# Edge attention on a graph: four batches to a period, Q and E by edge, and one tie of the gathers to TensorE per period

## The chip, the cores and the metric

The kernel runs on one core of one Trainium2 chip. The time is device microseconds of one execution. Engine names are those of the profile: PE is TensorE's matmuls and PEld its weight loads, DVE is VectorE, ACT is ScalarE, POOL is GpSimd, and SP is SyncE, which here only issues DMAs. POOL issues the gathers, each an indirect DMA that fetches one row for each of 128 partitions.

## The reference

A graph has 6250 nodes with 128 features and 206250 edges, sorted by their destination `dst`. Every edge has 128 features of its own. With 8 heads of 16 features:

```python
Qh = (h @ WQ).reshape(N, H, D)
Kh = (h @ WK).reshape(N, H, D)
Vh = (h @ WV).reshape(N, H, D)
Eh = (edge_attr @ WE).reshape(-1, H, D)
score = jnp.einsum('ehd,ehd,ehd->eh', Kh[src], Qh[dst], Eh) * inv_sqrt_d
score = jnp.exp(jnp.clip(score, -5.0, 5.0))
msg = Vh[src] * score[:, :, None]
wV = jax.ops.segment_sum(msg, dst, num_segments=N)
Z = jax.ops.segment_sum(score, dst, num_segments=N)
h_out = wV / (Z[:, :, None] + 1e-06)
```

The output is `layernorm(x + h_out)` over the features. So for every edge, the row of K and V of its source is needed, the row of Q of its destination, and E of the edge. All data are float32.

## The kernel before

**Tiles.** The edges are cut into 1612 tiles of 128 edges, and these into 406 batches: 401 of four tiles, then five smaller ones. A batch `b` goes through stages, and each turn of the main loop (lines 464 to 516) works on several batches at different stages.

**Head.** `table` (lines 226 to 245) computes K and V of all nodes in 49 blocks of 128: one matmul into PSUM each (`kvacc`), a copy by ACT or DVE into `kvst`, and stores into the table `kv` in HBM. `q_rows` computes Q, split into three bfloat16 parts that add up to the float32 value, and stores it in `qs`. While the table is not there yet, the first 12 batches (`XB`) gather rows of `x` (512 bytes) instead of rows of `kv` (1 KB), and `project` computes their K and V on the spot.

**Stages of a batch.**
- `gather` (line 307): POOL issues four indirect DMAs into a tile `kvrows`; there are 17 such tiles (`GB`).
- `stage_0`: DVE compares each edge's destination with a row of numbers. `onehot` has the edges on the partitions, `onehotT` has the Q rows of a window of 42 nodes (times three parts) on them, in bfloat16.
- `stage_a`: PE multiplies the window's Q rows with `onehotT` (`qps`, line 354), one product of 512 columns, whose result has the features on the partitions and the edges along the row. ACT copies it to SBUF (`qT`, line 356). PE multiplies the edge features with WE in the same layout (`eps`, line 358).
- `pairs`: DVE multiplies `qT` with `eps` (`eq`, line 365). `turn`: PE transposes the four tiles of `eq` to have the edges on the partitions (`pps`, line 373).
- `stage_b`: DVE multiplies the gathered K rows with `pps` (`kq`, line 379), sums over each head (line 382) and clips (line 385). `weigh`: ACT takes the exponential twice, once into PSUM (`bank`) for the messages and once into the last eight columns of `msg`.
- `messages`: DVE multiplies the gathered V rows with the weights (`msg`, line 413). `stage_c`: PE multiplies `onehot` with `msg` and adds this up in PSUM over a group of 11 tiles (`agg`, line 431). After a group ACT copies the sum out (`sum`, line 441).
- When the groups that touch 128 nodes are there, `finish` adds them by PE with shifted identity matrices (`finps`, line 401), and `layernorm` makes some 17 small DVE operations, of which `fill()` issues one at a time between the others.

**What sets the order.** From batch 12 on, every engine keeps to the order of the program (`manual_schedule`). A float32 product is two instructions on PE. The gathers are tied to PE: the first of the four of batch `b`, from batch 16 on, waits for the `qps` product of batch `b - lag(b)`, where `lag` falls from 12 to 1 within the first 60 batches:

```python
if i == 0 and b >= LOCK:
    tc.add_manual_dep(ins.ins, expanded[b - lag(b)].ins.name, ...
```

SP's queue holds the loads of edge features (`ea`, 512 KB for 8 tiles), of the Q windows (`qw`), of `relb` (the destinations for `onehotT`), and the stores of the table, of Q and of the output.

Of the kernel before, what the change touches and what calls it, by code (L numbers as in the profile page):

```python
# [8 lines left out]
F32 = mybir.dt.float32  # L9
# [18 lines left out]
GB = 17  # L28
XB = 12
LOCK = XB + 4  # L30
STEP = 1
# [3 lines left out]
AHEAD = 2  # L35
EB = 6
SLAG = 2
# [6 lines left out]
QLOOK = 3  # L44
# [30 lines left out]
def q_built(j):  # L75

    return min(NB, (j * N // NJ + 3 * P - 1) // P)


@with_exitstack  # L80
def edge_attention(ctx: ExitStack, tc: tile.TileContext, x, xT, srcT, dstT, dstB, dst0, bnd, lo, eaT,
# [30 lines left out]
    with ExitStack() as fast:  # L112
# [78 lines left out]
        def count_inside():  # L191
# [9 lines left out]
            nc.vector.tensor_copy(cnt_i, pc)  # L201
# [5 lines left out]
        psE = fast.enter_context(tc.tile_pool(name="psE", bufs=1, space=bass.MemoryType.PSUM))  # L207
        psQ = fast.enter_context(tc.tile_pool(name="psQ", bufs=1, space=bass.MemoryType.PSUM))
        psP = fast.enter_context(tc.tile_pool(name="psP", bufs=2, space=bass.MemoryType.PSUM))
# [4 lines left out]
        bank = psX.tile([P, P + B * H], F32, name="bank")  # L214
        iota_p, exp_p = bank[:, :P], bank[:, P:].rearrange("p (b h) -> p b h", h=H)
        nc.vector.tensor_copy(iota_p, iota_f)

        def pair_bank(i, name, shape):

            pool, tag = ((psE, "eps"), (psP, "pps"), (psQ, "qps"), (psP, "pps"))[i % 4]  # L220
            return pool.tile(shape, F32, name=name, tag=tag)
# [4 lines left out]
        def table(b0):  # L226
            st = wp.tile([P, KB, 2 * D], F32, name="kvst", bufs=2)
            blocks = range(b0, min(NB, b0 + KB))
            for b in blocks:
                n = min(P, N - b * P)  # L230
                ps = pair_bank(b, "kvacc", [P, 2 * D])
                nc.tensor.matmul(ps[:n], xT_sb[:, LEFT + b * P:LEFT + b * P + n], wkv_sb,
                                 start=True, stop=True)
                if b % 2:
                    nc.vector.tensor_copy(st[:n, b - b0, :], ps[:n])
                else:
                    nc.scalar.copy(st[:n, b - b0, :], ps[:n])
# [5 lines left out]
            if len(full) < len(blocks):  # L243
                b = blocks[-1]
                nc.sync.dma_start(kv[b * P:N], st[:N - b * P, b - b0, :])

        batches = cut_batches()
        nbat = len(batches)
        manual = []
        xbs, stores, norms, pending, ready = {}, [], [], [], []  # L250
# [4 lines left out]
        def q_rows(q):  # L255
            n = min(P, N - q * P)
            ps = psT.tile([P, D], F32, name="qrows", tag="oT")
            nc.tensor.matmul(ps[:n], xT_sb[:, LEFT + q * P:LEFT + q * P + n], wq_sb, start=True, stop=True)
            st = wp.tile([P, QP, D], BF16, name="qst", bufs=1)
            r1 = wp.tile([P, D], F32, name="qr1", bufs=1)  # L260
            nc.scalar.copy(st[:n, 0, :], ps[:n])  # L261
            nc.vector.tensor_tensor(r1[:n], ps[:n], st[:n, 0, :], op=ALU.subtract)  # L262
            nc.scalar.copy(st[:n, 1, :], r1[:n])
            nc.vector.tensor_tensor(st[:n, 2, :], r1[:n], st[:n, 1, :], op=ALU.subtract)
            nc.sync.dma_start(qs[q * P * QP:(q * P + n) * QP].rearrange("(p s) f -> p s f", s=QP), st[:n])
            built.append(q)

        def load_q(j):
            if j >= NJ or j in loaded:
                return  # L270
            if j % QREG == 0:
# [4 lines left out]
            loaded[j] = wp.tile([QROWS, D], BF16, name="qw", bufs=QLOOK + 2)  # L276
            nc.sync.dma_start(loaded[j], qs[ds(regs[j % QREG], QROWS), :])

        def load_rel(c):
# [3 lines left out]
            rels[c] = wp.tile([QROWS, RC * P], BF16, name="relb", bufs=2)  # L283
# [3 lines left out]
        chunks, aggs, sums, st8, expanded = {}, {}, {}, {}, {}  # L287
# [9 lines left out]
        def ea_tiles(t, n):  # L297

            load_chunk(t // CH)
            j = t % CH * P  # L300
            return chunks[t // CH][:, j:j + n * P]

        def lag(b):

            return max(STEP, 12 - (b - LOCK) // 4)

        def gather(b):
            rows, f = (x, D) if b < XB else (kv, 2 * D)
            g = gp.tile([P, B, 2 * D], F32, name="kvrows")
            for i, t in enumerate(batches[b]):  # L310
# [6 lines left out]
                if i == 0 and b >= LOCK:  # L317
                    tc.add_manual_dep(ins.ins, expanded[b - lag(b)].ins.name,
# [4 lines left out]
        def project(g, n):  # L323
# [4 lines left out]
            xgT = wp.tile([P, B, P], F32, name="xgT", tag="kq", bufs=2)  # L328
            nc.scalar.copy(xgT[:, :n], pt[:, :n])
            for i in range(0, n, 2):  # L330
                k = min(2, n - i)
                pk = pair_bank(i // 2, "kvps", [P, 2, 2 * D])
# [4 lines left out]
        def stage_0(b):  # L337
            t0, n = batches[b][0], len(batches[b])
            oh = wp.tile([P, B, P], F32, name="onehot", bufs=AHEAD + 5)
# [328 lines left out]
```

## Time and profile before

Three executions took 2434.01, 2427.33 and 2426.94 us; the median is 2427.33 us.

| what | value |
|---|---|
| profiled execution | 2430.0 us, of which the profile's span is 2428.1 us |
| PE busy | 1539.8 us, 63% |
| DVE busy | 1577.4 us, 65% |
| POOL busy | 1534.0 us, 63% |
| ACT busy | 458.9 us, 19% |
| granted TensorE clock, mean | 0.811 |
| moved by DMA | 398.16 MB, mean 164 GB/s |

A line of the groups names the source line, the engine, the operation, its output and inputs with their shapes, and how often it ran; then the busy time in us, the mean of one in ns, and the engine's idle time just before these instructions with what ended most of it. "issue" is time in which an engine waited for nothing that the profile shows, and "remote" is a wait whose releaser it can't name. A line of the waits has, after the engine, the line and what ended the wait: us in total, times, and the longest in us.

### The profile page before, as it was taken

To read this page: it belongs to the slowest core of one execution; us is meant where nothing else is said; L and a number is where in the kernel's file an instruction comes from. 1 tells how busy PE (TensorE), PEld (TensorE's weight loads), DVE (VectorE), ACT (ScalarE), POOL (GpSimd) and SP (SyncE) were. 2 spreads that over 40 slices of the span, in tenths; PEclk is the share of its full clock that TensorE was granted. 3 is DMA by queue.
4 is the path that set the end of the run, shared out by engine and by line. 5 is a ranking of instruction groups with operands and counts; after the bars stand their busy time and mean duration, and the time that the engine had idled before them with its cause. 6 is when DMAs were issued, how large, how long until landed. Compare 5 with 4: busy or idle time off the path is not lost.

```text
span 2428.1 us, 24930 instructions
## 1 busy us (share of the span) xinstructions
PE 1539.8 (63%) x6880; PEld 1086.0 (45%) x6880; DVE 1577.4 (65%) x3779; ACT 458.9 (19%) x1572; POOL 1534.0 (63%) x1619
## 2 busy tenths in 40 slices
PE   3587666666665666657666666666666656656665
PEld 2365444444444444444444444444444444444444
DVE  1368778666766666667667666666666667666766
ACT  0232122111111111111111111111111111111111
POOL 7346565666666666666666666666666666666664
PEclk6898898887878888778877878788778788887887
DMA  5645555556554555556456554655555556554642
GB/s 176 201 144 174 179 156 178 165 150 185 170 166 148 168 177 156 164 152 196 147 157 196 160 156 149 184 168 151 169 162 178 147 155 196 157 156 146 197 150 71
DMA packets 178482, 398.16 MB, mean 164 GB/s; under 512 B 61756, under 2 KB 87526, under 8 KB 178336
## 3 DMA queue, kind: packets, MB, share of 16 engines
q0 software_dynamic: 76592, 208.18, 29.4%
q1 hardware_dynamic: 100604, 187.38, 25.2%
q8 instruction: 57, 0.93, 0.2%
q10 hardware_dynamic: 1140, 0.93, 0.1%
q14 instruction: 89, 0.73, 0.1%
HBM read 381.54 MB, written 14.81 MB: 163 GB/s over the span
## 4 chain that ended last, share of the span: by engine, by line
PE 34%; another core or an unknown queue 23%; DVE 19%; issue 16%; ACT 4%; DMA 2%; POOL 1%; DVEq 1%; SPq 0%; ACTq 0%; POOLq 0%
PE agg L431 10%; PE eps L358 10%; PE pps L373 7%; DVE sc L382 4%; DVE kq L379 4%; DVE eq L365 3%; PE qps L354 3%; ACT qT L356 2%; DVE msg L413 2%; PE finps L401 2%; POOL kvrows L314 1%; DVE onehot L340 1%; DVE onehotT L344 1%; DMA kvrows<-kv,src 1%
## 5 line engine op out<-in xcount | busy, mean ns | idle before, releaser
L314 POOL DMA_INDIRECT kvrows<-kv,src x1564 | 1487.1, 951 | 862.3 <-issue 385.6
L431 PEld LDWEIGHTS agg<-msg,onehot 128*128 128x128 f32 x3224 | 516.7, 230 | 664.3 <-issue 520.9
L431 PE MATMUL agg<-msg,onehot 128*128 128x136 f32 x3224 | 560.5, 326 | 352.8 <-DVE msg L413 137.2
L373 PE MATMUL pps<-shift,eq 128*128 128x128 f32 x1612 | 320.5, 332 | 419.6 <-DVE eq L365 238.5
L365 DVE TENSOR_TENSOR eq<-qT,eps 128x512 f32<-128x512 f32 x406 | 276.4, 681 | 476.2 <-ACT qT L356 210.9
L358 PE MATMUL eps<-ea,we_sb 128*128 128x512 f32 (+1 forms) x812 | 528.2, 738 | 16.8 <-issue 13.4
L373 PEld LDWEIGHTS pps<-shift,eq 128*128 128x128 f32 x1612 | 221.4, 168 | 477.4 <-DVE eq L365 282.4
L356 ACT COPY qT<-qps 128x512 f32<-128x512 f32 x406 | 236.8, 583 | 1048.5 <-remote 428.8
L379 DVE TENSOR_TENSOR kq<-kvrows,pps 128x512 f32<-128x512 f32 x406 | 274.8, 677 | 12.1 <-remote 3.5
L413 DVE TENSOR_TENSOR msg<-kvrows,bank 128x512 f32<-128x512 f32 x406 | 274.6, 676 | 9.8 <-ACT bank L391 4.3
L382 DVE TENSOR_REDUCE sc<-kq 128x32 f32<-128x512 f32 x406 | 276.0, 680 | 7.3
L340 DVE TENSOR_TENSOR onehot<-bank,dst_sb 128x512 f32<-128x512 f32 x406 | 275.8, 680 | 0.0
L358 PEld LDWEIGHTS eps<-ea,we_sb 128*128 128x128 f32 x812 | 192.1, 238 | 50.0 <-issue 14.6
L354 PE MATMUL qps<-onehotT,qw 126*128 126x512 bf16 x406 | 187.3, 461 | 0.9 <-ACT qT L356 0.9
L344 DVE TENSOR_SCALAR onehotT<-relb,node 126x512 bf16<-126x512 bf16 x406 | 147.0, 363 | 16.7 <-remote 11.2
L391 ACT ACTIVATE bank<-sc 128x32 f32<-128x32 f32 x406 | 83.0, 204 | 257.2 <-DVE onehot L340 139.8
L401 PEld LDWEIGHTS finps<-sum,shift 128*128 128x128 f32 x478 | 73.1, 215 | 62.4 <-issue 33.9
L401 PE MATMUL finps<-sum,shift 128*128 128x136 f32 x478 | 75.8, 307 | 30.9 <-ACT sum L441 26.2
L262 DVE TENSOR_TENSOR qr<-qrows,qst 128x128 f32<-128x128 f32 (+1 forms) x49 | 14.2, 289 | 116.8 <-ACT qst L261 104.4
L393 ACT ACTIVATE msg<-sc 128x32 f32<-128x32 f32 x406 | 88.0, 217 | 0.0
L385 DVE TENSOR_SCALAR sc<-sc 128x32 f32<-128x32 f32 x406 | 79.2, 195 | 7.3
L441 ACT COPY sum<-agg 128x136 f32<-128x136 f32 x146 | 39.3, 269 | 236.2 <-remote 100.7
(66 smaller groups left out, 525.9 us busy)
## 6 DMA issues: line engine op xcount, KB each, us to landing
ea<-eaT SPq DMA_DIRECT2D x201, 512.0 KB
relb<-relD SPq DMA_DIRECT2D x100, 504.0 KB
kvrows<-kv,src POOLq DMA_INDIRECT x1564
qw<-qs SPq DMA_DIRECT2D x202, 31.5 KB
kv<-kvst SPq DMA_DIRECT2D x12, 512.0 KB
qs<-qst SPq DMA_DIRECT2D x48, 96.0 KB
xb<-x SPq DMA_DIRECT2D x48, 64.0 KB
out<-h SPq DMA_DIRECT2D x48, 64.0 KB
```

Of the source, the lines that this page charges most:

```text
L314: ins = nc.gpsimd.indirect_dma_start(out=g[:k, i, :f], out_offset=None, in_=rows, in_offset=bass.IndirectOffsetOnAxis(ap=src_col(t)[:k], a ...
L340: nc.vector.tensor_tensor(oh[:, :n], iota_p[:, None, :].to_broadcast([P, n, P]), rel[:, t0:t0 + n, None].to_broadcast([P, n, P]), op=ALU.i ...
L354: expanded[b] = nc.tensor.matmul(pq[:, :n * P], loaded[t0 // WT], ohT[:, :n * P], start=True, stop=True)
L356: nc.scalar.copy(qT[:, :n * P], pq[:, :n * P])
L358: nc.tensor.matmul(pe[:, :n * P], we_sb, ea_tiles(t0, n), start=True, stop=True)
L365: nc.vector.tensor_tensor(eq[:, :n * P], qT[:, :n * P], pe[:, :n * P], op=ALU.mult)
L373: nc.tensor.transpose(pp[:, i, :], eq[:, i * P:i * P + P], ident)
L379: nc.vector.tensor_tensor(t1[:, :n], g[:, :n, :D], pp[:, :n], op=ALU.mult)
L382: nc.vector.tensor_reduce(sc[:, :n], t1[:, :n].rearrange("p b (h d) -> p b h d", h=H), axis=AX.X, op=ALU.add)
L401: nc.tensor.matmul(ps, shift[:, P - s:2 * P - s], sums[k], start=i == 0, stop=stop and i == len(parts) - 1)
L413: nc.vector.tensor_tensor(m[:, :n, :D].rearrange("p b (h d) -> p b h d", h=H), g[:, :n, D:].rearrange("p b (h d) -> p b h d", h=H), exp_p[ ...
L431: nc.tensor.matmul(aggs[k], oh[:, i, :], m[:, i, :], start=first and not final, stop=last)
```

## The change

The main loop takes **periods** of four batches (100 of them, for batches 0 to 399), then periods of one batch for the last six. Within a period:

1. `multiply` for each of the four batches: DVE multiplies the gathered K rows with the Q product and then the result with the E product, both read from PSUM. After each, `expand(b + 2)` orders PE's products for the batch two further on.
2. `weigh`, `messages` and `aggregate` for the four batches, one step apart.
3. `one_hot` for the four batches of the next period, and `one_hot_rows` for four batches.

Q and E are computed **by edge**: in `expand`, `onehotT` and the edge features are the stationary operands, tile by tile, and the results have the edges on the partitions. The copy `qT`, the multiply `eq` with it, and the transposes `pps` are gone. PSUM has two buffers each for `qps` and `eps`.

The gathers have **one tie a period**: the first of its 16 waits for the last `agg` product of the period `p - lag(p)`; from period 4 on, with lag 4 at first and 2 from period 12 on. There are 14 gather tiles in place of 17. The **x gathers**, 48 in number, are tied to `table`'s products from the third batch on. Three groups of sums share a PSUM bank and are copied out at once. The Q rows and the sums of 128 nodes are jobs: their PE products are ordered after the multiplies of a period, and the copies behind them in the next one. Stores are issued a period later; `ea` has 5 buffers in place of 6, `relb` 3 in place of 2.

```diff
-GB = 17
+GB = 14
 XB = 12
-LOCK = XB + 4
-STEP = 1
+PER = 4
+LOCK = XB // PER + 1
+STEP = 2
...
+        def lag(p):
+            return max(STEP, 4 - (p - LOCK) // 4)
+        def gather(b, p=0, made=None):
...
-                if i == 0 and b >= LOCK:
-                    tc.add_manual_dep(ins.ins, expanded[b - lag(b)].ins.name,
+                if i == 0 and p >= LOCK and b == periods[p][0]:
+                    made = added[p - lag(p)]
+                if i == 0 and made is not None:
+                    tc.add_manual_dep(ins.ins, made.ins.name,
...
+        def expand(b):
             t0, n = batches[b][0], len(batches[b])
             if b < XB:
-                project(g, n)
-            oh, ohT = st8.pop(b)
-            pq = psQ.tile([P, B * P], F32, name="qps")
-            expanded[b] = nc.tensor.matmul(pq[:, :n * P], loaded[t0 // WT], ohT[:, :n * P], start=True, stop=True)
-            qT = wp.tile([P, B * P], F32, name="qT", bufs=2)
-            nc.scalar.copy(qT[:, :n * P], pq[:, :n * P])
-            pe = psE.tile([P, B * P], F32, name="eps")
-            nc.tensor.matmul(pe[:, :n * P], we_sb, ea_tiles(t0, n), start=True, stop=True)
+                project(gathered[b], n)
+            ohT = hotT.pop(b)
+            pq = psQ.tile([P, B, D], F32, name="qps")
+            for i in range(n):
+                nc.tensor.matmul(pq[:, i, :], ohT[:, i * P:i * P + P], loaded[t0 // WT], start=True, stop=True)
+            pe = psE.tile([P, B, D], F32, name="eps")
+            for i in range(n):
+                nc.tensor.matmul(pe[:, i, :], ea_tile(t0 + i), we_sb, start=True, stop=True)
+            pairs[b] = pe, pq
...
+            nc.vector.tensor_tensor(t1[:, :n], g[:, :n, :D], pq[:, :n], op=ALU.mult)
+            fill()
+            nc.vector.tensor_tensor(t1[:, :n], t1[:, :n], pe[:, :n], op=ALU.mult)
...
-        gathered = {b: gather(b) for b in range(min(XB, len(batches)))}
+        gathered = {b: gather(b) for b in range(2)}
         for b0 in range(0, NB, KB):
-            table(b0)
+            made = table(b0)
...
+            for b in range(len(gathered), min(XB, nbat)):
+                if (b - 2 if b < 5 else b) * KB > b0:
+                    break
+                gathered[b] = gather(b, made=made)
...
+            for b in c:
+                multiply(b)
+                step()
+                if b + EA < nbat:
+                    expand(b + EA)
+            while job:
+                step()
+            if p == 15:
+                pc = count_inside()
+            else:
+                new_job(c)
+            for i in range(len(c) + 1):
+                if i < len(c):
+                    weigh(c[i], i)
+                    fill()
+                if i:
+                    messages(c[i - 1], i - 1)
+                    aggregate(c[i - 1], p)
+                    fill()
...
+            for b in periods[p + 1] if p + 1 < len(periods) else ():
+                one_hot(b)
+                fill()
+            while next_row[0] < min(nbat, c[-1] + 1 + EA + (len(periods[p + 1]) if p + 1 < len(periods) else 0)):
+                one_hot_rows(next_row[0])
+                next_row[0] += 1
+                fill()
```

## The prediction

> **What bounds the kernel now.** I read the busy line first, then the chain, the costliest groups, all waits by engine, and last the timelines of POOL, ACT and PE side by side.
>
> ```profile
> PE 1539.8 (63%) x6880; PEld 1086.0 (45%) x6880; DVE 1577.4 (65%) x3779; ACT 458.9 (19%) x1572; POOL 1534.0 (63%) x1619
> ...
> PE 34%; another core or an unknown queue 23%; DVE 19%; issue 16%; ACT 4%; DMA 2%; POOL 1%; DVEq 1%; SPq 0%; ACTq 0%; POOLq 0%
> ...
> L314 POOL DMA_INDIRECT kvrows<-kv,src x1564 | 1487.1, 951 | 862.3 <-issue 385.6
> L431 PE MATMUL agg<-msg,onehot 128*128 128x136 f32 x3224 | 560.5, 326 | 352.8 <-DVE msg L413 137.2
> L373 PE MATMUL pps<-shift,eq 128*128 128x128 f32 x1612 | 320.5, 332 | 419.6 <-DVE eq L365 238.5
> L358 PE MATMUL eps<-ea,we_sb 128*128 128x512 f32 (+1 forms) x812 | 528.2, 738 | 16.8 <-issue 13.4
> L356 ACT COPY qT<-qps 128x512 f32<-128x512 f32 x406 | 236.8, 583 | 1048.5 <-remote 428.8
> L379 DVE TENSOR_TENSOR kq<-kvrows,pps 128x512 f32<-128x512 f32 x406 | 274.8, 677 | 12.1 <-remote 3.5
> ```
>
> No engine is full by its busy share, and 23% of the chain has no releaser that the profile knows. The gathers decide. Each of the 1564 from the kv table takes 0.951 us, and the next one starts 0.306 us after it even when nothing is late:
>
> ```profile
> POOL kvrows L314 <- issue: 399.9, 1306, 1.0
> ...
> POOL kvrows L314 <- DMA relb<-relD: 32.5, 1, 32.5
> ```
>
> 399.9 / 1306 = 0.306, so a gather costs 1.257 us. Busy 1487.1, plus 1564 x 0.306 = 479, plus 351 of longer pauses is 2317 us, and the POOL timeline shows just that stretch: from 96.2 (after the 32.5 us wait for the table) to 2412.2. The 351 us are what can be won there. The POOL timeline has 171 such pauses (gaps above 0.6 us): 351 / 171 = 2.05 us each beyond the usual gap, after runs of mostly 12, 8 or 4 gathers. Why POOL pauses is seen in three timelines of one stretch (start, us, engine, instruction, idle before):
>
> ```profile
> 1193.44 0.38 PE L354 MATMUL qps<-onehotT,qw 126*128 126x512 bf16 x1
> ...
> 1200.54 0.63 PE L354 MATMUL qps<-onehotT,qw 126*128 126x512 bf16 x1
> ```
> ```profile
> 1197.41 0.59 ACT L356 COPY qT<-qps 128x512 f32<-128x512 f32 x1 [4.93 <-remote]
> ...
> 1204.54 0.59 ACT L356 COPY qT<-qps 128x512 f32<-128x512 f32 x1 [6.30 <-PE agg L431]
> ```
> ```profile
> 1201.40 0.95 POOL L314 DMA_INDIRECT kvrows<-kv,src  x1 [0.31 <-issue]
> 1204.77 0.94 POOL L314 DMA_INDIRECT kvrows<-kv,src  x1 [2.43 <-PE agg L431]
> ```
>
> The product of 1193.44 has ended at 1193.82, but ACT's copy starts 3.6 us later; that of 1200.54 is picked up at 1204.54, 2.3 us after POOL went still, and POOL itself, tied to that product, goes on at the same moment. So TensorE's results are learned of late by the others while gathers are issued back to back, and all at once some 2.3 us after the gathers stop. By the same comparison 198 of the 406 qps copies start over 1 us after their product. No such lateness is seen between DVE and ACT. The cause I can't read from the trace; the regularity I use.
>
> **The change, part by part.** (1) *One tie per 16 gathers instead of one per 4.* A period is 16 x 1.257 = 20.1 us of gathers. If each tie ends a run, it costs 2.1 us (row above): 22.2 us a period, where four batches now take 2317 / 391 x 4 = 23.7. From below, a tie already met costs nothing (20.1). From above, DVE decides (rival C). I take the pause: the nearest rows are the runs of 12, which nearly all end in one. 97 periods carry kv rows: 97 x 20.1 = 1951, 97 x 2.1 = 204.
>
> (2) *Is the work of a period hidden under its gathers?* DVE is busy 1577.4 / 406 x 4 = 15.5 us per four batches. The edit keeps its count: eq (681 ns, qT from SBUF) becomes a second multiply (g x Q, then x E: nearest row 677), reduce, clip, messages, one-hots and layernorm steps are the same. What is new is where it stands. TensorE's Q and E of a period's batches 0 and 1 are ordered in the period before; those of 2 and 3 only behind the multiplies of 0 and 1. After 16 gathers, DVE finishes multiplies 2 and 3 (2 x 1.36 us), then does weights, messages and one-hots of the period (some 10 us), then multiplies 0 and 1 of the next: about 15.5 us into the next run. Batches 2 and 3 then need TensorE results that, late as now, come 2.3 us after the run ends. DVE stands from 15.5 to 22.2 and goes on: its loop closes in the same 22.2 us. The last sum (added) of that period lies about 11 us into a run; the tie with lag 2 asks for it at the end of that run, so nothing waits longer. Queued behind the waiting multiply on DVE is the whole weigh stage, and behind it ACT's Exp and PE's sums; all fit in. Cost: nothing, hidden by 20.1 us of gathers; without that cover it is rival C.
>
> (3) *TensorE.* Gone: 1612 transposes, 320.5 us. The E product becomes 3224 half-instructions with 128 columns in place of 812 with 512: by the nearest row (agg, same size) 3224 x 560.5 / 3224 = 560 against 528, +32. Q becomes 1612 bf16 products in place of 406: between 187 (as now) and 320 (a transpose each), I take 320, +133. Sum -155 us of 1540; PE is not the bound, so 0. The Trainium skill speaks against it ("TensorE: Matmul & The Clock Gate", Back-to-back issue gap): a stream of 128-column products costs about 81 ns each, of 512 columns about 131, so four small ones cost 2.5 large. By the page E goes from 812 x 0.131 = 106 to 3224 x 0.081 = 261 us, +155 in place of +32. The trace has 528 / 812 = 650 ns and 174 ns, so here the ratio is near four columns for four; the row is used. The same page (What's actually happening) has the clock halved after some 3.4 us without work, and PE will idle during one-hots. The trace shows both speeds: two 512-wide E instructions take 1.02 or 1.92 us, granted clock 0.81 on average. All at half speed, one batch's Q and E would take some 12 x 0.23 = 2.8 us (agg at its slow pace) against the 1.36 us of a multiply, and the four multiplies stretch by about 2.8 us; 15.5 + 2.8 = 18.3, still under 22.2. By full clock 15.5. Both give the same end.
>
> (4) *ACT* loses 406 qT copies (236.8 us) and gets one copy per three sums for 146 single ones. It is 19% busy; 0. Its wait for qps (428.8 us remote) moves to DVE, counted in (2).
>
> (5) *Head.* In the table phase the 48 x gathers run without a break until 63.7, and the table's copies crawl at one per 5.5 us each on ACT and DVE until they stop:
>
> ```profile
> 53.31 0.37 ACT L237 COPY kvst<-kvacc 128x256 f32<-128x256 f32 x1 [10.83 <-remote]
> 64.50 0.37 ACT L237 COPY kvst<-kvacc 128x256 f32<-128x256 f32 x1 [10.82 <-remote]
> ...
> 70.85 0.65 ACT L237 COPY kvst<-kvacc 128x256 f32<-128x256 f32 x2 [1.18 <-PE qrows L258]
> ```
>
> Tied to the table, they must pause about ten times (10 x 2.1 = 21 us; 48 x 1.257 = 60), and the table goes along: both end near 80 instead of 63.7 and 88. The kv gathers start between 75 and 96 (as before); I take 85. Then 14 buffers and lag 4 (periods 4 to 7) let POOL go on only at a period's first messages, i.e. after the late multiplies: 22.2 + 2 x 1.36 + about 1.7 = 26.6. Five such periods cost 22 us (bounds 0 and 60).
>
> (6) *Tail.* Now 16 us from the last gather. The last six batches (12 gathers) are periods of one with lag 2, so a tie asks for work just begun: first about 12 us behind the last full run, then two hops of some 8 us, then sums and layernorm, 12: 40 (between 25 and 60), with the 15 us of gathers in it. SP's loads and stores move by a period at most; the DMA queues are busy 55%; 0.
>
> Sum: 85 + 1951 + 204 + 22 + 40 = 2302 us span. The profiled run of before has 2430.0 around a span of 2428.1, so 1.9 more: 2304; it lies 2.7 above the median 2427.33, so I say **2303**.
>
> **Rivals.** *B, ties cost nothing* (results arrive on time when DVE no longer needs four of them in 20 us): 2303 - 204 = about 2100. For: a tie of two periods back is long met. Against: runs of 12 end in a pause though theirs was often old too.
>
> *C, slower: DVE becomes the bound* at multiplies 2 and 3. For: runs of 16 are longer than any kv run now, the waits of a period come in two steps (product 3 is ordered behind multiply 1, and the sums copy and the q job wait for PE as well), and late results have kept DVE's eq up to 5.3 us:
>
> ```profile
> DVE eq L365 <- remote: 162.8, 55, 5.3
> ```
>
> If the period's DVE work doesn't lie beside the lateness but ahead of it, a period is 15.5 us plus what DVE stands. Equal time is (2427 - 85 - 22 - 40 - 2) / 97 = 23.5 us, so it decides from 8.0 us of standing, two waits of 4. At two waits of 4.7 us (24.9 a period) it is 2415 + 149 = about 2560. Against: the second result has come by the time the first is delivered.
>
> *D, the gain is eaten:* pauses after 16 gathers take 3.4 us instead of 2.1, or head and tail cost 70 more: about 2420, on either side of no change.
>
> **How the numbers follow.** Likeliest, 0.46: 2303, its own range 2240 to 2370 (pause 1.6 to 2.7, head and tail within their bounds). B 0.12, C 0.30, D 0.12. About 0.3% is what a measurement tells from no change, 7 us. Faster: 0.46 + 0.12 + half of D = 0.64; within: 0.04; slower: 0.32. The range 2150 to 2510 leaves out most of B (0.09) and the worse third of C (0.11).
>
> **What would show it.** Right: POOL's timeline in runs of 16 with gaps of 2 to 2.7 us, period 22; DVE's second to fourth multiply waiting until about 2 us after POOL stops; weigh, messages and one-hots without gaps; PE busy near 1390. B: no gaps at 16. C: POOL gaps over 4 us, released by agg, and DVE busy without a break between a late multiply and the sums. Wrong above all if lateness grows with the run, or if it isn't tied to gathers at all: then results would be late after POOL stopped, too.

## The result, and the profile after

The changed kernel takes 2628.83 us (median of four executions, 2625.43 to 2631.02) against 2427.14 us before (2422.90 to 2434.01): a ratio of 1.083, 95% interval 1.0805 to 1.0855. The forecast was 2303 us. The profiled execution took 2631.02 us with a span of 2629.2 us.

The lines of the page that answer to those of before: busy time, the chain, and the groups (busy us, mean ns | idle before in us, and what ended most of it).

```profile
PE 1466.5 (56%) x8886; PEld 1298.8 (49%) x8886; DVE 1603.7 (61%) x3779; ACT 231.2 (9%) x1070; POOL 1529.5 (58%) x1619
...
issue 40%; PE 34%; DVE 13%; another core or an unknown queue 5%; ACT 1%; DMA 1%; POOL 0%; DVEq 0%; SPq 0%; ACTq 0%; POOLq 0%
...
L326 POOL DMA_INDIRECT kvrows<-kv,src x1564 | 1482.9, 948 | 1058.1 <-PE agg L455 448.4
L455 PE MATMUL agg<-msg,onehot 128*128 128x136 f32 x3224 | 739.0, 357 | 1034.9 <-issue 942.3
L375 PE MATMUL eps<-we_sb,ea 128*128 128x128 f32 x3224 | 538.9, 319 | 20.8 <-issue 15.2
L372 PE MATMUL qps<-qw,onehotT 126*128 126x128 bf16 x1612 | 191.3, 251 | 40.2 <-issue 17.5
```

A gather costs what it did. POOL's idle time grew from 862.3 to 1058.1 us, and now a named releaser ends most of it: `agg`, the sum to which the gathers are tied. POOL's timeline has 95 runs of exactly 16 gathers; the pauses after them sum to 564.2 us, 5.94 us each, where 2.36 were forecast (2.05 beyond the usual gap of 0.31). The median period is 25.7 us, not 22.2.

The new thing stands in the second group: TensorE's sums were idle 942 us ahead of themselves for "issue", a wait for nothing that the profile shows. In one period (timelines of POOL, PE and PEld; start, us, instruction, idle before):

```profile
1313.91 0.95 POOL L326 DMA_INDIRECT kvrows<-kv,src  x1 [0.30 <-issue]
1321.39 0.95 POOL L326 DMA_INDIRECT kvrows<-kv,src  x1 [6.54 <-PE agg L455]
```
```profile
1302.15 1.19 PE L455 MATMUL agg<-msg,onehot 128*128 128x136 f32 x8
...
1310.53 0.38 PE L455 MATMUL agg<-msg,onehot 128*128 128x136 f32 x1 [1.00 <-issue]
1311.96 0.38 PE L455 MATMUL agg<-msg,onehot 128*128 128x136 f32 x1 [1.04 <-issue]
1314.06 0.39 PE L455 MATMUL agg<-msg,onehot 128*128 128x136 f32 x1 [1.72 <-issue]
...
1317.56 3.56 PE L455 MATMUL agg<-msg,onehot 128*128 128x136 f32 x15 [0.31 <-issue]
1320.91 0.63 PE L372 MATMUL qps<-qw,onehotT 126*128 126x128 bf16 x4
```
```profile
1309.84 0.29 PEld L455 LDWEIGHTS agg<-msg,onehot 128*128 128x128 f32 x1 [1.10 <-issue]
1311.25 0.29 PEld L455 LDWEIGHTS agg<-msg,onehot 128*128 128x128 f32 x1 [1.12 <-issue]
```

This run of gathers began at 1295.00. At 1302.15 eight half-products of a batch take 1.19 us. From 1304 on each takes a slot of its own, loads and products in turn, about 0.7 or 1.4 us apart, though the profile shows nothing that they wait for. The last gather starts at 1313.91; 2.7 us after it has ended TensorE is back at its pace, finishes the sums at 1321.1, and only then POOL may go on. The counts by stretch show the two speeds (columns: stretch, its length, busy us and instructions of PE, PEld, DVE, ACT, POOL, then granted clock, DMA share, GB/s):

```profile
1295.00:1303.00 8.00, 8.00 (x63) 7.79 (x62) 6.92 (x14) 0.86 (x6) 6.16 (x7) 0.81 0.72 191
1303.40:1317.40 14.00, 3.21 (x9) 2.57 (x10) 6.79 (x14) 0.35 (x2) 8.72 (x10) 0.68 0.51 163
```

125 TensorE instructions in 8 us, then 19 in 14 us: 15.6 and 1.4 per us. DVE and ACT have no such thing; DVE stands 7.49 us there for a copy by ACT, and ACT 12.54 us, until 1317.74, for a product of TensorE that had ended at 1302.2: the late news of the prediction, beside the crawl. The crawl was to be read in the trace of before, as the first line of all its waits, which the prediction passed over because the chain gave "agg" only 10%:

```profile
PEld agg L431 <- issue: 520.9, 371, 10.8
```

In the changed kernel that line reads:

```profile
PEld agg L455 <- issue: 1033.0, 790, 3.3
```

### The profile page after: what moved, and what is told of

Read it like the earlier page. It is cut to its first block, busy times and chain, and to the rows that moved or that the text cites. A ratio compares the mean times of both kernels' runs of the same rounds, so it can differ in the third digit from the quotient of the medians.

```text
span 2629.2 us, 28306 instructions
## 1 busy us (share of the span) xinstructions
PE 1466.5 (56%) x8886; PEld 1298.8 (49%) x8886; DVE 1603.7 (61%) x3779; ACT 231.2 (9%) x1070; POOL 1529.5 (58%) x1619
## 4 chain that ended last, share of the span: by engine, by line
issue 40%; PE 34%; DVE 13%; another core or an unknown queue 5%; ACT 1%; DMA 1%; POOL 0%; DVEq 0%; SPq 0%; ACTq 0%; POOLq 0%
PE agg L455 20%; PE eps L375 10%; DVE sc L393 3%; PE qps L372 3%; DVE msg L411 3%; DVE kq L385 2%; DVE kq L383 1%; PE finps L406 1%; DVE sc L395 1%; DVE onehot L354 1%; ACT bank L396 1%; DVE onehotT L361 0%; POOL kvrows L326 0%; DMA ea<-eaT 0%
## 5 line engine op out<-in xcount | busy, mean ns | idle before, releaser
L326 POOL DMA_INDIRECT kvrows<-kv,src x1564 | 1482.9, 948 | 1058.1 <-PE agg L455 448.4
L455 PE MATMUL agg<-msg,onehot 128*128 128x136 f32 x3224 | 739.0, 357 | 1034.9 <-issue 942.3
L455 PEld LDWEIGHTS agg<-msg,onehot 128*128 128x128 f32 x3224 | 598.8, 248 | 1159.1 <-issue 1033.0
L375 PE MATMUL eps<-we_sb,ea 128*128 128x128 f32 x3224 | 538.9, 319 | 20.8 <-issue 15.2
L375 PEld LDWEIGHTS eps<-we_sb,ea 128*128 128x128 f32 x3224 | 480.9, 228 | 31.0 <-issue 20.0
L385 DVE TENSOR_TENSOR kq<-kq,eps 128x512 f32<-128x512 f32 x406 | 276.8, 682 | 116.0 <-remote 43.5
L383 DVE TENSOR_TENSOR kq<-kvrows,qps 128x512 f32<-128x512 f32 x406 | 271.1, 668 | 102.9 <-PE qps L372 72.6
L354 DVE TENSOR_TENSOR onehot<-bank,dst_sb 128x512 f32<-128x512 f32 x406 | 250.0, 675 | 0.0
L372 PE MATMUL qps<-qw,onehotT 126*128 126x128 bf16 x1612 | 191.3, 251 | 40.2 <-issue 17.5
L372 PEld LDWEIGHTS <-onehotT 126*128 126x128 bf16 x1612 | 154.6, 116 | 57.8 <-issue 38.6
L326 POOL DMA_INDIRECT kvrows<-x,src x48 | 45.6, 951 | 27.4 <-issue 13.1
```

Of the source, the lines that this page charges most:

```text
L326: ins = nc.gpsimd.indirect_dma_start(out=g[:k, i, :f], out_offset=None, in_=rows, in_offset=bass.IndirectOffsetOnAxis(ap=src_col(t)[:k], a ...
L354: nc.vector.tensor_tensor(hot[b][:, :n], iota_p[:, None, :].to_broadcast([P, n, P]), rel[:, t0:t0 + n, None].to_broadcast([P, n, P]), op=A ...
L372: nc.tensor.matmul(pq[:, i, :], ohT[:, i * P:i * P + P], loaded[t0 // WT], start=True, stop=True)
L375: nc.tensor.matmul(pe[:, i, :], ea_tile(t0 + i), we_sb, start=True, stop=True)
L383: nc.vector.tensor_tensor(t1[:, :n], g[:, :n, :D], pq[:, :n], op=ALU.mult)
L385: nc.vector.tensor_tensor(t1[:, :n], t1[:, :n], pe[:, :n], op=ALU.mult)
```

## The experiments

Theory after the result: beside an unbroken run of gathers TensorE does about 120 to 170 instructions and then crawls at about 1.4 per us until the gathers stop. A period of the changed kernel has 171 of them (matmuls and loads, counted in the trace; 160 of Q, E and sums), and they must be done within the run and its pause. Rivals: results are only told late (the prediction's view); memory traffic; a chain of DVE and PE by the order of the stages (rival C).

The runs fell on several chips, and this matters more than anything else in the case. On one chip the kernel before took 2427 to 2445 us (medians of two occasions), as in the first measurement, which names no chip. On four others it took 2043 to 2046 us. Each run below is compared with the kernel before on its own chip; "the slowed chip" is the one, "the other chips" are the four.

### The slowing by itself

A kernel without the computation: stretches parted by barriers, in each a stream of products that wait for nothing. Its stretches in short (`small(160)` is 160 float32 products of 128 columns, `wide(40)` 40 of 512):

```diff
+    small(160)                      # alone
+    gathers(24, rows, 256); small(160)
+    gathers(24, x, 128);    small(160)
+    gathers(24, rows, 256); [20 DVE operations]; small(160, after them)
+    gathers(24, rows, 256); wide(40)
+    [12 loads of 512 KB by SP]; small(160)
+    [16 memsets by POOL]; small(160)
+    gathers(24, rows, 256); [60 DVE and 60 ACT operations]; small(160)
```

> Leaves out the whole computation: stretches parted by barriers, in each TensorE has a stream of 160 float32 products of 128x128x128 (320 matmul and 320 load instructions) that wait for nothing, and beside it runs: nothing; 24 gathers of 1 KB rows; 24 gathers of 512 B rows; 24 gathers of 1 KB with the TensorE stream starting some 13 us late; 24 gathers of 1 KB with 40 products of 512 columns; 12 loads of 512 KB by SP and no gathers; POOL busy with memsets and no gathers; 24 gathers with DVE and ACT streams of 60 operations too. Theory (gathers starve TensorE): alone about 640 instructions in 40 to 75 us; beside gathers 8 us at that pace, then about 1.4 instructions per us until 3 us after the last gather; loads and memsets change nothing; DVE and ACT go on at their own pace. If it is a time since the run began, the late stream crawls from its first instruction; if it is a stock of instructions, its first 100 run at full pace. Rival (results are only told late): all TensorE streams take the same time. Rival (memory traffic): the loads by SP slow TensorE too, and 512 B rows less than 1 KB rows.

On the slowed chip, busy time by stretch (same columns as above): alone; then the first 9 us beside 1 KB gathers, the rest of these, and what follows them.

```profile
7.00:45.00 38.00, 37.75 (x320) 37.56 (x320) 0.00 (x0) 0.11 (x1) 0.00 (x0) 1.00 0.00 1
45.30:54.30 9.00, 9.00 (x82) 9.00 (x83) 0.00 (x0) 0.00 (x0) 6.87 (x8) 1.00 0.31 89
54.30:78.30 24.00, 8.30 (x32) 6.17 (x31) 0.00 (x0) 0.00 (x0) 15.96 (x17) 0.59 0.35 98
78.30:104.00 25.70, 25.29 (x209) 25.14 (x208) 0.00 (x0) 0.00 (x0) 0.00 (x0) 0.92 0.00 1
```

165 instructions in 9 us, then 63 in 24 us, then nearly full pace again: no wait for an operand or a PSUM buffer is involved. The clock isn't the start of it: it was granted in full until 58.7 us, over 3 us into the crawl, and came down after. Nor is it the loading of TensorE's instructions: the trace's queue for them (q8, read packet by packet) moves one packet per about 256 of them, at 47.05 us and next at 84.09, when the pace had come back. The crawl began and ended between the two.

And from the other stretches: 40 wide products beside gathers, SP's loads, POOL's memsets, and DVE and ACT beside gathers (two rows: ahead of the crawl and in it).

```profile
228.90:258.60 29.70, 29.70 (x70) 13.20 (x71) 0.00 (x0) 0.00 (x0) 22.66 (x24) 1.00 0.36 101
263.40:299.50 36.10, 35.97 (x320) 35.81 (x320) 0.00 (x0) 0.00 (x0) 0.00 (x0) 1.00 0.48 176
299.70:335.60 35.90, 35.90 (x320) 35.75 (x320) 0.00 (x0) 0.00 (x0) 28.76 (x16) 1.00 0.00 1
335.90:344.40 8.50, 8.50 (x76) 8.45 (x76) 7.91 (x18) 8.09 (x14) 6.63 (x7) 1.00 0.30 82
344.40:369.00 24.60, 6.40 (x22) 4.89 (x21) 20.91 (x43) 23.39 (x39) 17.21 (x18) 0.59 0.35 101
```

Loads at 176 GB/s (more than the gathers move) and a busy POOL slow nothing, so neither the bytes moved nor POOL's work as such does it. (Plain loads issued by POOL ran on the other chips alone, so whether it must be gathers isn't shown.) Rows of 512 B gave the same crawl (60.6 us for the stream, against 59.0 with 1 KB). DVE and ACT keep their pace in the crawl. The late stream, started 10 us into the gathers, did about 121 instructions before it crawled, and the wide products, 141 instructions in the 30 us of gathers, never did. So it isn't the time since the gathers began. The four streams that crawled did so after 121 to 174 TensorE instructions, and about 9 to 10 us after they began. The wide stream speaks against a time alone, but its 141 instructions lie within that range and came at 4.7 per us; whether a number or a rate decides isn't shown.

Two further kernels of this kind, run four times in all, were to show what ends the crawl (runs of 8, memsets between, POOL still) and whether copies of TensorE's results come late. All fell on the other chips.

```diff
+    gathers(24, rows, 256); small(160)          # not in the first of the two
+    gathers(24, rows, 256); wide(40), each copied out by ACT
+    [gather, memset] x 24; small(160)
+    [8 gathers, POOL waits 3 us] x 3; small(160)
+    [8 gathers, 2 memsets] x 3; small(160)
+    [24 plain loads of 128 KB by POOL]; small(160)
+    gathers(24, rows, 256); 160 (then 320) bf16 products
```

> Leaves out the whole computation, as the first such kernel, with other stretches: (1) 24 gathers of 1 KB beside 40 products of 512 columns, each copied out by ACT; (2) gathers parted by a memset of 1.8 us on POOL each, beside 160 small products; (3) runs of 8 gathers parted by about 3 us in which POOL only waits; (4) runs of 8 parted by two memsets, 3.6 us in which POOL works; (5) 24 plain loads of 128 KB by POOL; (6) gathers beside 160 bf16 products (320 instructions). Theory (a stock of some 120 to 170 TensorE instructions, hardly refilled while gathers are issued back to back, refilled when POOL stops issuing them): (1) products at full pace, but the copies fall behind late in the stretch, by several us, as in the kernel; (2) to (4) no or a far shorter crawl; (6) the crawl after about 150 instructions. If POOL must be still and not only issue no gathers, (2) and (4) crawl and (3) does not. (5) tells whether plain loads by POOL do it as well: no opinion. Rival (the late news is a matter of its own): (1) copies late though TensorE keeps its pace; the theory can't tell.

> Leaves out the whole computation. Stretches parted by barriers: (1) 24 gathers of 1 KB beside 160 small products; (2) 24 gathers beside 40 products of 512 columns, each copied out by ACT; (3) gathers parted by a memset of 1.8 us each; (4) runs of 8 gathers parted by about 3 us in which POOL only waits; (5) runs of 8 parted by two memsets; (6) 24 plain loads of 128 KB by POOL; (7) gathers beside 320 bf16 products (640 instructions). On a chip where the kernel before takes 2043 us: TensorE at full pace in all, as in the second such kernel. On one where it takes 2427 us: (1) the crawl after about 150 instructions, as in the first such kernel; (2) copies late by several us toward the end; (3) to (5) no crawl or a short one if POOL's rest lets TensorE catch up, and (3) and (5) like (1) if only idleness does; (7) as (1).

The second of them was run twice more:

> Leaves out the whole computation; the same stretches as in the third such kernel: gathers beside small products; beside wide products copied out by ACT; parted by memsets; in runs of 8 with POOL still for 3 us; in runs of 8 with two memsets; plain loads by POOL; beside bf16 products. Where the kernel before takes 2427 us: (1) a crawl after about 150 instructions; (2) copies late by several us toward the end; (3) to (5) no crawl or a short one if an end of gather issue lets TensorE catch up, (3) and (5) like (1) if POOL must be idle; (7) as (1). Where it takes 2043 us: 36 to 38 us in each, as before.

> Leaves out the whole computation; the same stretches as in the third such kernel: gathers beside small products; beside wide products copied out by ACT; parted by memsets; in runs of 8 with POOL still for 3 us; in runs of 8 with two memsets; plain loads by POOL; beside bf16 products. Where the kernel before takes 2427 to 2445 us: (1) a crawl after about 150 instructions; (2) copies late by several us toward the end; (3) to (5) no crawl or a short one if an end of gather issue lets TensorE catch up, (3) and (5) like (1) if POOL must be idle; (7) as (1). Where it takes 2043 us: 36 to 38 us in each, as before.

On four different chips nothing crawled. The first stretch is the one that took 59 us on the slowed chip:

```profile
6.70:44.90 38.20, 38.03 (x320) 37.84 (x320) 0.00 (x0) 0.00 (x0) 22.84 (x24) 1.00 0.29 83
```

All 640 instructions in 38 us, in what the stream took alone. The late news was absent as well: in all four runs each copy by ACT began 0.04 us after its wide product, with the gathers beside it. What ends the crawl, other than the end of the gathers, wasn't seen.

### Fewer TensorE instructions in the changed kernel

E and Q by one product of 512 columns for a batch, 22 instructions in place of 40, all else as it was. It leaves out the layout by edge, so the scores aren't those of the reference.

```diff
-            for i in range(n):
-                nc.tensor.matmul(pq[:, i, :], ohT[:, i * P:i * P + P], loaded[t0 // WT], ...)
+            nc.tensor.matmul(pq (as 512 columns), loaded[t0 // WT], ohT[:, :n * P], ...)
-            for i in range(n):
-                nc.tensor.matmul(pe[:, i, :], ea_tile(t0 + i), we_sb, ...)
+            nc.tensor.matmul(pe (as 512 columns), we_sb, chunks[t0 // CH][:, j:j + n * P], ...)
```

> The changed kernel, but E and Q of a batch by one product of 512 columns each, as in the kernel before: 22 TensorE instructions a batch (matmuls and loads) in place of 40; DVE, ACT, POOL and all waits as in the changed kernel. It leaves out the layout that the multiply needs. Theory (TensorE starves beside gathers, and the count of its instructions decides): pauses after 16 gathers fall from 5.9 to about 2.5 us, 2629 - 97 x 3.4 = about 2300 us. Rival (order of the stages or late results): the same waits, 2600 to 2640 us.

On the slowed chip: 2400.14 us, ratio to before 0.9885 (0.9853 to 0.9917). The same gathers, waits, DVE and ACT, and 229 us less than the changed kernel. POOL's pauses after 16 are 3.71 us on average (median 3.27), and the last sum of a period ends 11.7 us (median) after its run of gathers began; in the changed kernel 24.8 us. The sums' wait for "issue" fell to a tenth, and POOL's line of the waits shows what is left (us in total, times, longest):

```profile
PEld agg L457 <- issue: 103.2, 132, 2.6
```
```profile
POOL kvrows L326 <- remote: 243.9, 75, 3.7
```

These 3.3 us are the late news of the prediction: the sum to which the gathers are tied was done 8 us before the run ended, and POOL learned of it after it had stopped. The theory holds in direction; its 2300 was too low by 100 us, as the pauses took 3.7 us and not 2.5, with this news in most of them.

### Shorter runs in the changed kernel

```diff
-PER = 4
+PER = 2
-STEP = 2
+STEP = 3
...
```

(What is left out sets numbers of buffers.)

> The changed kernel with periods of two batches, one tie for 8 gathers, lag 3. Theory (TensorE starves late in a run): 8 gathers take 10.1 us, its 80 instructions fit into the first 8 to 10 us and the pause; pauses of about 2.2 us or less, so 20.1 + 2 x 2 = 24 us for four batches against 26 now: about 2480 us. Rival (the stages of a period are a chain on DVE and PE): more, shorter chains, each with its own wait for the exponential and for results: 2700 us.

On the slowed chip: 2466.74 us, ratio 1.0165 (1.0134 to 1.0196); 162 us less than with periods of four. POOL's timeline has 101 runs of 8 with pauses of 2.37 us and 46 of 16 with 4.25: now and then a tie is met in time and two periods run together. The theory's 2480 was near, and the chain of stages (2700) is out. Shorter runs also have fewer TensorE instructions in each, so this doesn't tell which of the two matters.

### Half the bytes

```diff
-            rows, f = (x, D) if b < XB else (kv, 2 * D)
+            rows, f = x, D
...
-                g[:, :n, D:].rearrange("p b (h d) -> p b h d", h=H),
+                g[:, :n, :D].rearrange("p b (h d) -> p b h d", h=H),
```

It leaves out the projection of later rows to K and V.

> The changed kernel with all gathers from x, 512 B a row in place of 1 KB: half the bytes, as many gathers and descriptors. It leaves out the projection of these rows to K and V for batches past the twelfth (the messages read the first half of the row). Theory (the issue of gathers starves TensorE): pauses stay at 5 to 6 us, about 2600 us. Rival (memory traffic of the gathers does it): pauses fall to about 2 us, about 2250 us.

On the slowed chip: 2615.81 us in one execution, pauses of 5.95 us. The bytes of the gathers don't matter; the number of rows fetched was the same and wasn't varied.

### The two halves of the change in the kernel before

The tie on every fourth batch alone:

```diff
-                if i == 0 and b >= LOCK:
+                if i == 0 and b >= LOCK and b % 4 == 0:
...
-STEP = 1
+STEP = 4
```

It was run four times, the last on the slowed chip:

> The kernel before with the tie on every fourth batch alone (lag 4 from there on), so runs of 16 gathers; nothing else. Theory: 120 TensorE instructions for 16 gathers lie between the changed kernel (160, pauses of 5.9 us) and the one with wide products (88, 3.5 us): pauses of 4.6 us, 20.1 + 4.3 = 24.4 us for four batches, 97 x 24.4 + 116 = about 2480 us. Rival (fewer ties are fewer pauses of 2.1 us, as predicted): about 2300 us.

> The kernel before with the tie on every fourth batch alone (lag 4), as already run on the other chip, where it made no difference (2042 against 2043 us). Where the kernel before takes 2427 us. Theory (TensorE starves late in a run, by the count of its instructions): 120 instructions for 16 gathers lie between 88 and 160: pauses of about 4.6 us, about 2480 us. Rival (fewer ties are fewer pauses of 2.1 us, as predicted): about 2300 us. Where it takes 2043 us: 2042 us again.

> The kernel before with the tie on every fourth batch alone (lag 4). Where the kernel before takes 2427 us (TensorE slowed beside gathers). Theory (the count of TensorE's instructions between pauses decides): 120 for 16 gathers lie between 88 (pauses 3.7 us) and 160 (5.9 us): pauses of about 4.6 us, about 2480 us. Rival (fewer ties are fewer pauses of 2.1 us, as predicted): about 2300 us. Where it takes 2043 us: no difference.

> The kernel before with the tie on every fourth batch alone (lag 4). Where the kernel before takes 2427 us (TensorE slowed beside gathers). Theory (the count of TensorE's instructions between pauses decides): 120 for 16 gathers lie between 88 (pauses 3.7 us) and 160 (5.9 us): pauses of about 4.6 us, about 2480 us. Rival (fewer ties are fewer pauses of 2.1 us, as predicted): about 2300 us. Where it takes 2043 us: no difference.

On three of the other chips it made no difference: 2042.25 against 2043.06 us (ratio 0.9999, 0.9990 to 1.0007), 2042.65 (0.9996) and 2043.80 (0.9998). On the slowed chip: 2832.96 us against 2444.98, ratio 1.1602 (1.1569 to 1.1636). Both forecasts for it fell, by far. Waits of this kernel there:

```profile
POOL kvrows L314 <- PE qps L354: 738.7, 96, 22.7
ACT qT L356 <- remote: 675.7, 88, 15.4
PEld pps L373 <- DVE eq L365: 646.7, 178, 14.4
DVE eq L365 <- remote: 559.8, 75, 13.7
```

Pauses after 16 are 7.7 us (median 6.3), longer than in the changed kernel though a period has a quarter fewer TensorE instructions. So the count isn't all. TensorE's own waits hardly grew against the kernel before: the sums' line for "issue" was 520.9 us there and is here

```profile
PEld agg L431 <- issue: 513.5, 351, 13.7
```

and that of `pps` went from 187.2 to 230.8. What grew are the "remote" waits of the first list, for results that TensorE had finished: of `qT` from 428.8 to 675.7 us (the longest from 8.9 to 15.4) and of `eq` from 162.8 to 559.8 (from 5.3 to 13.7). So in this kernel it is the news that came later with the longer run, more than TensorE that crawled more. Every batch here has three legs on TensorE, one after the other, with a copy or a multiply between (`qps` to `qT`, `eq` to `pps`, messages to `agg`), and each can be caught in the same run. The changed kernel asks for Q and E ahead of time and has one leg less; that it is 204 us faster than this one is in line with that, but one run doesn't part the reasons.

Q and E by edge alone (no `qT`, `eq` by feature or transposes; ties each batch, lag 2; two PSUM buffers each, and the later stages a turn earlier):

```diff
-            expanded[b] = nc.tensor.matmul(pq[:, :n * P], loaded[t0 // WT], ohT[:, :n * P], ...)
-            nc.scalar.copy(qT[:, :n * P], pq[:, :n * P])
-            nc.tensor.matmul(pe[:, :n * P], we_sb, ea_tiles(t0, n), ...)
+            for i in range(n):
+                expanded[b] = nc.tensor.matmul(pq[:, i, :], ohT[:, i * P:i * P + P], loaded[t0 // WT], ...)
+            for i in range(n):
+                nc.tensor.matmul(pe[:, i, :], ea_tiles(t0 + i, 1), we_sb, ...)
...
-            nc.vector.tensor_tensor(t1[:, :n], g[:, :n, :D], pp[:, :n], op=ALU.mult)
+            nc.vector.tensor_tensor(t1[:, :n], g[:, :n, :D], pq[:, :n], op=ALU.mult)
+            nc.vector.tensor_tensor(t1[:, :n], t1[:, :n], pe[:, :n], op=ALU.mult)
```

> The kernel before with Q and E by edge alone: no qT copy, no eq by feature, no transposes; g x Q and then x E a turn earlier; ties each batch at lag 2 in place of 1, so that a gather has as much time as before. 40 TensorE instructions a batch (matmuls and loads) in place of 30. Theory (their count decides): slower, 2470 to 2560 us. Rival (this half of the change is a gain, the periods and the tie lose it): 2380 to 2420 us.

> The kernel before with Q and E by edge alone, as already run on the other chip, where it took 2047 against 2043 us. Where the kernel before takes 2427 us. Theory (the count of TensorE's instructions decides, 40 a batch in place of 30): 2470 to 2560 us. Rival (the periods and the tie lose it): 2380 to 2420 us. Where it takes 2043 us: 2047 us again.

> The kernel before with Q and E by edge alone, ties each batch. Where the kernel before takes 2427 us. Theory (the count decides, 40 instructions a batch in place of 30): 2470 to 2560 us. Rival (the periods and the tie lose it, this half is a gain): 2380 to 2420 us. Where it takes 2043 us: 2047 us.

> The kernel before with Q and E by edge alone, ties each batch at lag 2. Where the kernel before takes 2427 to 2445 us (TensorE slowed beside gathers). Theory (the count decides, 40 instructions a batch in place of 30): 2480 to 2600 us. Rival (the longer run alone loses it, by edge is a gain or nothing): 2380 to 2440 us. Where it takes 2043 us: 2047 us.

All four of its runs fell on the other chips: 2046.95, 2048.13, 2049.04 and 2049.44 us, ratios 1.0018 to 1.0023 with intervals within 1.0011 to 1.0032. So there this half costs 0.2%; what it does on the slowed chip wasn't measured.

### Fewer instructions in the kernel before

Sums in bf16, messages split into a high and a low half; one product of 272 columns a tile in place of two of 136, 22 instructions a batch in place of 30.

```diff
...
+            nc.scalar.copy(mm[:, :n, 0, :], m[:, :n])
...
+            nc.vector.tensor_tensor(mm[:, :n, 1, :], m[:, :n], mm[:, :n, 0, :], op=ALU.subtract)
...
-                nc.tensor.matmul(aggs[k], oh[:, i, :], m[:, i, :], ...)
+                nc.tensor.matmul(aggs[k], oh[:, i, :], m[:, i].rearrange("p s f -> p (s f)"), ...)
```

> The kernel before with the sums in bf16: the messages split in a high and a low bf16 half (one copy by ACT and one subtraction by DVE a batch more), one product of 272 columns a tile in place of two of 136; 22 TensorE instructions a batch in place of 30; 16 gather tiles in place of 17. Theory: fewer and shorter pauses, 2300 to 2390 us. Rival (DVE or the order decides): 0.6 us of DVE and of ACT a batch more, 2430 to 2550 us.

It fell on one of the other chips: 2137.88 against 2043.06 us, ratio 1.0468 (1.0451 to 1.0485). There TensorE's count has nothing to give. The trace shows where the 95 us went: a gather took 0.985 us on average in place of 0.949 (about 57 us over 1612), POOL made 16 pauses (37 us in all), and the tail was 6 us longer; why the gathers were dearer wasn't tested. Whether fewer instructions help on the slowed chip stays open.

### The changed kernel where nothing is slowed

> The changed kernel once more, unaltered. In the last runs the kernel before took 2043 us on another chip, with its gathers in one run of 1399 and no pause, where it had taken 2427. If the chip of this run is of that kind (kernel before near 2043): the gathers decide there, 20.1 us for four batches in both kernels, and the changed one pays only for its tail of single periods: 2040 to 2110 us. If it is of the first kind (kernel before near 2427): 2630 us again.

On one of the other chips: 2057.51 against 2043.72 us, ratio 1.0069 (1.0050 to 1.0088). As in the forecast there, the gathers decide: POOL has 1604 of them in two runs, the second of 1412, from 3.7 to 2019.0 us, and the period's ties aren't felt. (The kernel before left no trace on this chip; with one tie in four batches it has no pause over 0.6 us there.) What is left is the tail; POOL's timeline at the end:

```profile
2018.05 0.94 POOL L326 DMA_INDIRECT kvrows<-kv,src  x1 [0.30 <-issue]
2026.19 0.94 POOL L326 DMA_INDIRECT kvrows<-kv,src  x1 [7.19 <-PE qps L372]
2027.44 1.04 POOL L326 DMA_INDIRECT kvrows<-kv,src  x1 [0.30 <-issue]
2030.06 0.94 POOL L326 DMA_INDIRECT kvrows<-kv,src  x1 [1.58 <-PE agg L455]
...
2042.05 0.90 POOL L326 DMA_INDIRECT kvrows<-kv,src  x1 [2.62 <-PE agg L455]
```

The single periods wait for each other: 37.3 us from the end of the last full run to the end of the span at 2056.3, with 8 gathers in them. In the kernel before with one tie in four batches, on the same chip, POOL goes through to 2024.1, and the span ends 14.4 us later.

No version that computes all of it was clearly faster than the kernel before where it was measured, on either kind of chip.

## Why the prediction was wrong

**The step that failed** is the second, "Is the work of a period hidden under its gathers?", in its sentence that the last sum "lies about 11 us into a run; the tie with lag 2 asks for it at the end of that run, so nothing waits longer". It took TensorE at its own pace and only its news as late. The last sum of a period ended 24.8 us after the run's start, about 5 us after the last gather of the run, because TensorE itself crawled beside the gathers (19 instructions in 14 us). With fewer TensorE instructions and the same order, it ended at 11.7 us: the order of the stages was worked out right, TensorE's speed was not. The term of the sum is the pause: 97 x 2.1 = 204 us against about 95 x (5.94 - 0.31) = 535 for the full runs, 331 more. The whole miss of the span is 2629 - 2302 = 327. Of it, 229 us went with the fewer TensorE instructions. The other 98 stayed, with pauses of 3.71 us: most of them end in late news of 3.3 us after 16 gathers, where 2.36, usual gap included, was taken from shorter runs.

**The gathers** (1951 us) cost what was said: 948 ns and the gap of 0.3. **The head** held: x gathers until 74.6, the first from the table at 83.3 (85 forecast). **The tail** took 47.8 us from the end of the last full run on the slowed chip and 37.3 on another; 40 was said. **DVE** kept its count and stood from about 15.5 us into the run, as worked out (its first multiply of the period at 1309.88, 14.9 us after 1295.00); it stood 7.5 us, for ACT's copy of a sum and not for Q and E as forecast, and this isn't what POOL waited for. **TensorE's sum** was -155 us; busy time fell by 73, with the sums (`agg`) 178 us dearer, in the crawl and at a mean granted clock of 0.723 in place of 0.811 (492.0 us on another chip, against 739.0). Q cost 191, not the 320 taken; E 539, near the 560 taken from the trace's row and nothing like 2.5 times the 528 of before, the other ratio weighed there.

**Rival C** had the sign, and with 24.9 us a period against 25.7 nearly the size, but not the place: it put the wait on DVE's third and fourth multiply, and it was TensorE's sums. The mark given for it, pauses above 4 us released by `agg`, was there; DVE "busy without a break" was not. That it came near is luck.

**The warning** at the end, "wrong above all if lateness grows with the run", named what happened, but it bore no price in the range: runs of 16 were costed at the pause of runs of 12. With the tie moved alone, the slowed chip went from 2445 to 2833 us, so the rarer tie by itself is a loss of 16% there and not the gain of 147 us (351 of pauses before, 204 after) that was the heart of the forecast; and there it was the lateness that grew. On the other chips there was nothing to gain: the gathers of the kernels traced there hardly pause.

**Slips** that bear on nothing: 2304 less 2.7 is 2301 and not 2303; 70 us more of head and tail, in rival D, is 2373 and not 2420; and the table's copies came one per 5.5 us from ACT and DVE together, as the two lines from ACT alone lie 11.2 us apart.

**Open:** what slows TensorE, and why on one chip of five, or whether it is that chip and not what else ran beside it; whether E and Q by edge alone would be a gain or a loss on the slowed chip; and whether the late news and the crawl are one thing. They are found together and missing together: in the kernel before on the slowed chip 198 of 406 copies `qT` began over 1 us after their product, and in that kernel with one tie in four, in each of its three runs on the other chips, 1 of 406. That the news was late in the kernel with wide products, with the sum long done, and the crawl came in a stream that waits for nothing, shows only that each can be seen without the other. One rival was left untested: every execution was recorded by the profiler, so whether recording TensorE's many instructions has a part in the slowing isn't known.

## What to carry to other kernels

When results of an engine seem to be told late, first look whether that engine itself is slowed: its own waits for "issue", and its instructions per us in windows along the stretch, say it in two lines. Then work out, before making a stretch longer, what that engine must do within it and how often another engine must hear of it: both grew dear here. And measure the kernel before on more than one chip before spending effort on a wait: here the whole question, gain and loss, existed on one in five.

## What the runs showed of the hardware

- Beside an unbroken run of indirect gathers issued by POOL, TensorE on one chip did 121 to 174 instructions and then about 1 to 2.6 per us (63 in 24 us) until 3 to 4 us after the last gather (2.7 us in the changed kernel). Not by bytes (512 B rows the same), not by loads of 176 GB/s from SP's queue, not by POOL's memsets; DVE and ACT kept their pace.
- At 4.7 TensorE instructions per us (wide products, 141 in 30 us), gathers brought no crawl.
- On the same chip TensorE's results reached ACT and POOL late while gathers ran: a sum done 8 us before the end of a run reached POOL 3.3 us after that end (kernel with wide products), and ACT waited up to 15.4 us for `qps` (one tie in four). On the four others ACT's copy of a wide product began 0.04 us after it.
- The same kernel differed by 19% between chips (2427 to 2445 against 2043 to 2046 us), with the same cost of a gather (0.95 us and a gap of 0.30) on both.
- POOL issued up to 1612 gathers without a pause over 0.6 us. At 1.25 us each, the 1564 from the table take 1955 us: an estimate of the least this kernel can take, as long as each tile has a gather of its own.
